# Two graph attention layers: another queue for one block's softmax sums, and a first node block in two parts

## The chip, the cores and the metric

The kernel runs on one core of a Trainium2 chip, in one launch. The metric is the device time of a run in microseconds (us); lower is better. All data are float32, except for a copy of the adjacency matrix that the kernel keeps in DRAM as one byte per element.

The engines are named as in the profile: PE is the matrix engine (PEld its weight loads), DVE the vector engine, ACT the scalar engine, POOL the GpSimd, SP the sync engine, which computes nothing here and issues transfers.

## The reference, cut to what matters

There are 4096 nodes with 512 features, and an adjacency matrix of 4096 x 4096. Two layers follow each other; H = 4 heads of D = 128 features each.

```python
# layer 0
h  = relu(layernorm(x))
Xw = einsum('hnd,hde->hne', heads(h), W)
f1, f2 = Xw . V[:, 0], Xw . V[:, 1]
att = softmax over neighbours of sigmoid(f1[:, :, None] + f2[:, None, :])
Xn  = batchnorm(att @ Xw)                       # the encoder's attention
emb = batchnorm(elu(Xn @ Wenc.T + b) + Xn)
Y   = elu((att @ emb_heads) @ W.T)              # the decoder's attention, the same weights
x   = x + batchnorm(elu(Y @ Wdec.T + b) + Y)
# layer 1
h     = relu(layernorm(x))
feats = einsum('nf,hfo->hno', h, W1)            # "the last layer's values"
e_s, e_n = feats . a_self, feats . a_neigh
attn  = softmax over neighbours of leaky_relu(e_s[:, :, None] + e_n[:, None, :])
x     = x + relu(attn @ feats + b)
```

A softmax's denominator is, for each target node, the sum of the unnormalized weights over its neighbours. The kernel multiplies unnormalized weights by the values and scales the result by the inverse of the denominator afterwards.

## The kernel before

**The encoder's attention.** Its function `attention` goes over 8 blocks: 4 heads times 2 halves of 2048 targets (`TB`). A block has 32 iterations `j`, one for each 128 source nodes. An iteration makes a tile `e` of 128 x 2048 weights: ACT computes a Tanh (L572) and an Exp (L573), DVE multiplies by the adjacency tile `a` (L574). PE then adds `e` times the values of these sources into four banks of PSUM (L470). The tile `a` is one byte per element and has five buffers; SP loads it (`load_mask`, L213) from the byte copy in DRAM, which eight large transfers on POOL's queue make out of the float adjacency (`copy_adjacency`, L603) while the features and the first block are computed.

**The sums.** The denominators of a block are collected in three ways, set for each block by a list of iterations: some weight tiles are summed on DVE into `acc` (L500), some are added by POOL's transfers into a second sum (L490), some go through PE against a tile of ones (L268). The first block (n = 0) uses no POOL transfers for sums. In the second block (n = 1) the iterations 12, 14, 17, 19, 22, 24 and 26 go by POOL.

**From sum to scale.** The denominators of a block are finished during the next block. `ending` puts its steps into that block's iterations with `at(j, ...)`: evict the products (`out_enc`), copy the sums out of PSUM and store them to DRAM (`denominators`, iteration 4: DVE L274, transfer L275), load them back as 128 columns of 16 (`columns`: transfer L280 into `dcol`), invert them on DVE (`invert_them`: L284, L285), store the inverses (`inverses`, L288), load them over all partitions (`spread`, L293), and scale (L688). In the encoder all these transfers are on POOL's queue (`hop = nc.gpsimd`). For the first block alone `slack` is 4, which puts the inversion and all after it four iterations later: the inversion in iteration 14.

**The order of the work.** The code's order is not the engines' order. A planner goes through the program with modelled durations and, for each engine, issues what is ready, the earlier in the program first; the order it finds is then fixed for each engine, and semaphores keep it right. `tc.issue_after(x)` holds instructions behind `x` on `x`'s own engine. The steps put in by `at` are held behind the weights of the iteration before (`pinned(products_of)`), whose last instructions are on ACT and DVE; a transfer issued by SP is not held by that. Each engine, SP and POOL included, takes its instructions strictly in the fixed order, and a transfer that reads what another wrote waits on its issuing engine until that one has landed.

**The last layer's values.** After the decoder's MLP, `residual(o, ib)` finishes 128 features `o` of 512 nodes `ib`: ACT scales (L870), DVE adds the input (L871). Sums over the features go into `S[ib]`. For the layernorm, PE multiplies `S` by a matrix of 1/512 (`mean_of`), which puts each node's mean on all partitions; `centred(ib)` subtracts it on DVE (L931), ACT takes the Relu (L935) and the squares (L934, L938), DVE adds the squares up (L939, L940), and `deviation` turns them into 1/std through PE again (L946). `values` multiplies the Relu by the weights `w1x`, 128 nodes at a time (L957). For the first 512 nodes (`ib == 0`) `S` holds three of the four feature blocks, and a second product adds the fourth (L919 and L920). Just before, PE does the small products of the weights with the attention vectors (L903) and, between them, four products that nobody reads (`stay_busy`, L121). `w1x`'s last columns are copied behind the residual (L922).

Of the kernel before, what the change touches and what calls it, by code (L numbers as in the profile page):

```python
# [31 lines left out]
FP = mybir.dt.float32  # L32
U8 = mybir.dt.uint8
AF = mybir.ActivationFunctionType
# [5 lines left out]
N, F, H, D, P = 4096, 512, 4, 128, 128  # L40
IB = 512
NIB = N // IB
NJ = N // P
C = IB // P
# [32 lines left out]
INVERT = 4  # L77
# [13 lines left out]
def kernel(ctx, tc, x, xT, adjT, w0, w0T, v0, wencT, wdecT, vecs, w1, w1T, a1, outT):  # L91
    nc = tc.nc
# [12 lines left out]
    def nodes(r, ib):  # L105
        return r[:, ib * IB:(ib + 1) * IB]
# [4 lines left out]
    def bank():  # L111
        return psum.tile([P, IB], FP, name="ps")

    def bank1():
        return psum1.tile([P, IB], FP, name="den")

    def stay_busy(behind, n=1, cols=IB):

        for _ in range(n):
            with tc.issue_after(behind.ins):  # L120
                behind = nc.tensor.matmul(bank()[:, 0:cols], ident, w0Ts.rearrange("p h d -> p (h d)")[:, 0:cols],  # L121
                                          start=True, stop=True)
        return behind
# [30 lines left out]
    bias = consts.tile([P, C], FP, name="bias")  # L154
# [69 lines left out]
    def attention(what, keep, pools, weights, values, row_of, out, finish, ebufs, modes=None, invert=None,  # L224
# [38 lines left out]
        hop = nc.scalar if kept is None else nc.gpsimd  # L263
# [4 lines left out]
                last_ones = nc.tensor.matmul(den[s * 32:(s + 1) * 32, :], ones[:, 0:32], t[:, s * IB:(s + 1) * IB],  # L268
                                             start=start, stop=stop)

        def denominators(h, tb, den):

            dsb = spool.tile([P, IB], FP, name="dsb", tag="rb", bufs=3)
            (nc.vector.tensor_copy if kept is not None else nc.scalar.copy)(dsb, den)  # L274
            hop.dma_start(dens[h][tb], dsb[0:P:32, :])  # L275

        def columns(h, tb, dcols):

            dcol = spool.tile([P, TB // P], FP, name="dcol", bufs=2)
            hop.dma_start(dcol, dens[h][tb].rearrange("s (q k) -> (s q) k", k=TB // P))  # L280
            dcols.append(dcol)
# [8 lines left out]
        def spread(h, tb, s):  # L290

            rb = spool.tile([P, IB], FP, name="rb", bufs=3 if fast is None else 2)
            hop.dma_start(rb, everywhere(rinvs[h][tb], 0, s * IB, IB))  # L293
            return rb

        def at(j, f, *args):

            later.setdefault(j, []).append(lambda: f(*args))

        def ending(h, tb, po, den, slack):  # L300

            outs = [out(spool, h, tb, s, po[s]) for s in range(SB)]
            if den is not None:

                dcols = []
                at(INVERT, denominators, h, tb, den)
                at(INVERT + (0 if hop is nc.gpsimd else 3), columns, h, tb, dcols)
                at(INVERT + slack + (6 if hop is nc.gpsimd else 7), invert_them, dcols)
                at(INVERT + slack + (6 if hop is nc.gpsimd else 10), inverses, h, tb, dcols)
            rbs = {}  # L310
            for s, o in enumerate(outs):

                j = INVERT + slack + (7 if hop is nc.gpsimd else 11) + s % 2 + s // 2 * (7 if hop is nc.gpsimd else 5)
                at(j, lambda s=s: rbs.update({s: spread(h, tb, s)}))
                for k, f in enumerate(finish):
                    at(j + (6 + k if hop is nc.gpsimd else 3 + 3 * k),
                       lambda f=f, s=s, o=o: f(spool, h, tb, s, o, rbs[s], False))
# [78 lines left out]
        for n, (h, tb) in enumerate(blocks):  # L396
            last = n == len(blocks) - 1
            moved, by_ones, *ends_later = modes(n) if modes is not None else ((), ())
            den = bank1() if invert is not None else None
# [135 lines left out]
            for s, b in enumerate(po):  # L535
                for part in last_parts(s):
                    for k, t in late:
                        nc.tensor.matmul(b[:, part], block(values[h], k), t[:, s * IB:(s + 1) * IB][:, part],
                                         start=(k == 0), stop=(k == NJ - 1 and part.stop == IB))
# [37 lines left out]
    a_att, b_att, a_mlp, b_mlp = (coefs[:, k, :] for k in range(4))  # L577

    with tc.tile_pool(name="keep", bufs=1) as keep:

        with tc.tile_pool(name="f_small", bufs=1) as small, tc.tile_pool(name="f_work", bufs=2) as work:
# [26 lines left out]
            for ib in range(NIB):  # L608
# [14 lines left out]
                hT = work.tile([P, C, IB], FP, name="hT")  # L623
                for c in range(C):
# [15 lines left out]
                    for fb in range(C):  # L640
                        last_pe = nc.tensor.transpose(pt[:, fb, :], hn[:, fb * P:(fb + 1) * P], ident)
                    nc.scalar.activation(hT[:, :, c * P:(c + 1) * P], pt, AF.Relu)
                if ib == 0:

                    pw = bank1()
                    with tc.issue_after(last_pe.ins):
                        for h in range(H):
                            nc.tensor.matmul(pw[:, 2 * h:2 * h + 2], w0Ts[:, h, :], v0s[:, h, :],
                                             start=True, stop=True)
# [4 lines left out]
                for c in range(C):  # L654
                    j = ib * C + c
                    for k in range(2):
                        pv = heads_of(bank())
                        for h in range(2):
                            nc.tensor.matmul(pv[:, h, :], hT[:, 2 * k + h, c * P:(c + 1) * P], w0x[:, 2 * k + h, :],
                                             start=True, stop=True)  # L660
# [196 lines left out]
    with tc.tile_pool(name="l_small", bufs=1) as small, tc.tile_pool(name="l_work", bufs=2) as work:  # L857
        x1 = [R[2]] + [small.tile([P, N], FP, name=f"x1_{o}") for o in range(1, C)]

        S = [small.tile([P, IB], FP, name=f"S{i}") for i in range(NIB)]  # L860
# [2 lines left out]
        a1s = small.tile([P, H, 2], FP, name="a1s")  # L863
        nc.scalar.dma_start(a1s, a1)

        def residual(o, ib):
            d = nodes(x1[o], ib)
            xt = work.tile([P, IB], FP, name="xt")
            nc.sync.dma_start(xt, xT[o * P:(o + 1) * P, ib * IB:(ib + 1) * IB])
            nc.scalar.activation(d, d, AF.Identity, bias=b_mlp[:, o:o + 1], scale=a_mlp[:, o:o + 1])  # L870
            added = nc.vector.tensor_add(d, d, xt)  # L871
            if o == 1:
                nc.gpsimd.tensor_add(S[ib], nodes(x1[0], ib), d)
            elif o == C - 2 or o == C - 1 and ib > 0:
                (nc.gpsimd if o < C - 1 else nc.vector).tensor_add(S[ib], S[ib], d)

            if o == C - 1:
                nc.sync.dma_start(nodes(outT[o * P:(o + 1) * P, :], ib), d)
            elif ib == NIB - 1:
                nc.sync.dma_start(outT[o * P:(o + 1) * P, :], x1[o])  # L880
            return added

        def between(o, ib, made):

            if o in (1, 2):
                residual(o - 1, ib)
            elif o == C - 1 and ib >= NIB // 2:
                residual(o - 1, ib - NIB // 2)
# [6 lines left out]
        for fb in range(C):  # L895
            nc.scalar.dma_start(w1x[:, fb, :, 0:D], w1[fb * P:(fb + 1) * P, :].rearrange("p (h d) -> p h d", d=D))
        pw = bank1()
        last_pe = last_product
        for fb in range(C):
            with tc.issue_after(last_pe.ins):  # L900
                for h in range(H):
                    k = 2 * (fb * H + h)
                    last_pe = nc.tensor.matmul(pw[:, k:k + 2], w1Ts[:, h, fb * P:(fb + 1) * P], a1s[:, h, :],  # L903
                                               start=True, stop=True)
            last_pe = stay_busy(last_pe)
        mean_of = small.tile([P, P], FP, name="mean_of")
        nc.gpsimd.memset(mean_of, 1.0 / F)
        vacc = edge.tile([P, H, D], FP, name="vacc")

        def centred(ib):  # L910

            if ib >= NIB // 2:
                residual(C - 2, ib)
            added = residual(C - 1, ib)
            pm = bank()
            if ib == 0:

                with tc.issue_after(last_pe.ins):
                    nc.tensor.matmul(pm, mean_of, S[ib], start=True, stop=False)  # L919
                nc.tensor.matmul(pm, mean_of, nodes(x1[C - 1], ib), start=False, stop=True)  # L920
                with tc.issue_after(added.ins):
                    nc.vector.tensor_copy(w1x[:, :, :, D:DX],  # L922
                                          pw[:, 0:2 * C * H].rearrange("p (c h s) -> p c h s", h=H, s=2))
            else:
                nc.tensor.matmul(pm, mean_of, S[ib], start=True, stop=True)
            hT = work.tile([P, C, IB], FP, name="hT")
            sq = work.tile([P, C, IB], FP, name="sq", bufs=1)

            d = hT if ib else sq
            for fb in range(C):  # L930
                nc.vector.tensor_sub(d[:, fb, :], nodes(x1[fb], ib), pm)  # L931
            for fb in range(C):
                if ib:
                    nc.scalar.activation(sq[:, fb, :], d[:, fb, :], AF.Square)  # L934
                last_relu = nc.scalar.activation(hT[:, fb, :], d[:, fb, :], AF.Relu)  # L935
            if ib == 0:
                for fb in range(C):
                    nc.scalar.activation(sq[:, fb, :], d[:, fb, :], AF.Square)  # L938
            nc.vector.tensor_add(sq[:, 0:2, :], sq[:, 0:2, :], sq[:, 2:4, :])  # L939
            nc.vector.tensor_add(S[ib], sq[:, 0, :], sq[:, 1, :])  # L940
            return hT, last_relu
# [19 lines left out]


        hT, last_relu = centred(0)
        ahead = [values(hT, c) for c in range(2)]
        with tc.issue_after(ahead[-1][1].ins):
            rstd = deviation(0)
        for ib in range(NIB):
            for c in range(C):

                if c == (1 if ib else 2) and ib < NIB - 1:  # L970
                    with pinned([last_relu]):
                        hT_next, last_relu = centred(ib + 1)
# [22 lines left out]
            if ib < NIB - 1:  # L995
                hT, rstd = hT_next, deviation(ib + 1)
        last_pe = stay_busy(pvs_last, cols=IB // 2)
# [4 lines left out]
        with tc.issue_after(last_pe.ins):  # L1002
            last_pe = stay_busy(nc.tensor.transpose(pt[0:H, 0:P], mloc, ident), cols=IB // 2)
# [4 lines left out]
        pm = bank1()  # L1008
        with tc.issue_after(last_pe.ins):
            last_pe = nc.tensor.matmul(pm[:, 0:H], ones[0:H, :], mdiag, start=True, stop=True)  # L1010
# [16 lines left out]
    with tc.issue_after(last_pe.ins):  # L1027
        for h in range(H):
            last_pe = nc.tensor.matmul(pss[:, h:h + 1], vacc[:, h, :], ones[:, 0:1], start=True, stop=True)
    last_pe = stay_busy(last_pe, 3)  # L1030
# [104 lines left out]
```

## Time and profile before

| | us |
|---|---|
| median of 3 runs | 3187.92 (3186.09 to 3189.45) |
| the profiled execution's own time | 3189.23 |
| its span, first to last instruction | 3187.4 |
| PE busy | 3140.5 (99%) |
| DVE busy | 2934.3 (92%) |
| ACT busy | 2572.8 (81%) |
| POOL busy | 522.3 (16%) |

The span is 1.8 us shorter than the profiled execution's time. Busy times are sums over the whole span, and PE's is an upper bound, since matmuls are pipelined. A row of groups gives a line of the code, its engine, its operation, what it writes and reads, and then its count, busy time, mean duration and the idle time before it with what ended that. SPq and ACTq are the engines' own queues, in which transfers are issued. The granted clock of PE was 0.998 of full speed.

### The profile page before, as it was taken

What the parts mean: (1) busy time and instruction counts of PE and PEld (TensorE: products, weight loads), DVE (VectorE), ACT (ScalarE), POOL (GpSimd) and SP (SyncE); (2) the same over time, 40 slices, a digit from 0 to 9 for tenths busy, and PEclk for the clock granted to TensorE, in tenths of its full rate; (3) what the DMA queues carried; (4) which work ended last, traced back from release to release, by engine and by line L of the source; (5) the groups of instructions that cost most, each with busy time, mean ns of one, the idle gap of its engine ahead of it and who ended that gap; (6) DMA issues with size and microseconds to landing.
All of it is one profiled execution on the core that took longest, in us unless ns stands there. A gap on an engine that the chain in (4) does not pass through costs nothing.

```text
span 3187.4 us, 30095 instructions
## 1 busy us (share of the span) xinstructions
PE 3140.5 (99%) x10555; PEld 1371.4 (43%) x10555; DVE 2934.3 (92%) x2222; ACT 2572.8 (81%) x1825; POOL 522.3 (16%) x679
## 2 busy tenths in 40 slices
PE   7999999999999999999999999999999999999999
PEld 6334444444444463333333333458644444444444
DVE  7989999999998778999999999785699999999998
ACT  7999999999998449999999999456755666665663
POOL 3001211211211000010100100026312222122221
PEclk9999999999999999999999999999999999999999
DMA  9998978988987014444445454331579999999996
GB/s 212 199 194 252 265 209 232 269 222 228 267 227 205 20 44 149 155 155 159 159 162 165 145 169 145 90 112 57 158 189 232 214 225 237 218 216 236 230 210 174
DMA packets 215488, 590.30 MB, mean 185 GB/s; under 512 B 25928, under 2 KB 29288, under 8 KB 199336
## 3 DMA queue, kind: packets, MB, share of 16 engines
q0 software_dynamic: 70976, 231.94, 38.1%
q1 hardware_dynamic: 132344, 332.53, 30.4%
q10 hardware_dynamic: 12016, 23.90, 2.1%
q8 instruction: 83, 1.36, 0.2%
q14 instruction: 69, 0.57, 0.1%
HBM read 379.20 MB, written 84.30 MB: 145 GB/s over the span
## 4 chain that ended last, share of the span: by engine, by line
PE 73%; DVE 10%; ACT 7%; issue 7%; DMA 2%; DVEq 0%; ACTq 0%; POOL 0%; POOLq 0%
PE ps L470 32%; PE ps L332 22%; PE ps L724 7%; ACT e L572 4%; DVE e L574 4%; PE den L332 3%; PE ps L957 3%; DVE acc L500 3%; ACT e L573 2%; PE den L268 2%; DMA a<-mask 1%; DVE R L500 1%; DVE e L1052 1%; PE ps L806 1%; PE ps L467 1%
## 5 line engine op out<-in xcount | busy, mean ns | idle before, releaser
L470 PE MATMUL ps<-e,R 128*128 128x512 f32 x3992 | 1736.0, 595 | 22.5 <-DVE e L574 18.5
L470 PEld LDWEIGHTS ps<-e,R 128*128 128x128 f32 x3992 | 754.3, 190 | 1000.4 <-issue 924.0
L574 DVE TENSOR_TENSOR e<-e,a 128x2048 f32<-128x2048 f32 (+1 forms) x470 | 1049.6, 2261 | 77.7 <-ACT e L573 64.3
L572 ACT ACTIVATE e<-rowb,score 128x2048 f32<-128x2048 f32 (+1 forms) x470 | 909.0, 1969 | 20.2 <-PE ps L332 9.0
L573 ACT ACTIVATE e<-e 128x2048 f32<-128x2048 f32 (+1 forms) x470 | 866.6, 1879 | 8.3 <-DVE e L574 5.0
L332 PE MATMUL ps<-e,R 128*64 128x512 f32 x2624 | 746.8, 592 | 1.6 <-DVE e L574 1.5
L1051 ACT ACTIVATE e<-rowb,nq,jcol 128x2048 f32<-128x2048 f32 x224 | 459.3, 2088 | 264.1 <-DMA w<-e 137.1
L1052 DVE SCALAR_TENSOR_TENSOR e<-e,jcol,a 128x2048 f32<-128x2048 f32 (+1 forms) x265 | 591.2, 2262 | 2.8 <-ACT e L1051 2.8
L332 PEld LDWEIGHTS ps<-e,R 128*64 128x64 f32 x2624 | 241.9, 137 | 319.8 <-issue 316.2
L500 DVE TENSOR_TENSOR R<-R,e 128x2048 f32<-128x2048 f32 x124 | 282.2, 2276 | 0.0
L500 DVE TENSOR_TENSOR acc<-acc,e 128x2048 f32<-128x2048 f32 x122 | 278.6, 2284 | 1.0
L490 POOL DMA_DIRECT2D w<-e x178 | 149.1, 847 | 610.7 <-DMA w<-e 301.0
L724 PE MATMUL ps<-R,w 128*128 128x512 f32 x512 | 220.8, 592 | 0.6 <-DVE w L698 0.6
L490 POOL DMA_DIRECT2D acc<-e x142 | 119.1, 895 | 517.7 <-DMA acc<-e 199.1
L724 PEld LDWEIGHTS ps<-R,w 128*128 128x128 f32 x512 | 97.1, 190 | 123.0 <-issue 116.5
L332 PE MATMUL den<-e,R 128*64 128x512 f32 x320 | 149.8, 592 | 0.0
L332 PE MATMUL ps<-e,w 128*64 128x512 f32 x288 | 138.1, 592 | 0.7 <-DVE e L574 0.7
L293 POOL DMA_DIRECT2D rb<-rinvs x60 | 34.2, 573 | 519.3 <-DVE R L688 455.2
L957 PE MATMUL ps<-w1x,hT 128*128 128x260 f32 x512 | 115.5, 384 | 1.4 <-ACT hT L935 1.4
L332 PE MATMUL ps<-t,w 128*64 128x512 f32 x336 | 111.2, 592 | 1.0 <-DVE t L341 1.0
L957 PEld LDWEIGHTS ps<-w1x,hT 128*128 128x128 f32 x512 | 96.5, 190 | 19.9 <-issue 3.3
L332 PE MATMUL ps<-t,R 128*64 128x512 f32 x192 | 90.2, 592 | 0.0
(206 smaller groups left out, 2112.9 us busy)
## 6 DMA issues: line engine op xcount, KB each, us to landing
a<-mask SPq DMA_DIRECT2D x720, 256.0 KB, 4.2
w<-e POOLq DMA_DIRECT2D x178, 512.0 KB, 6.5
acc<-e POOLq DMA_DIRECT2D x142, 512.0 KB, 6.9
e<-ekeep SPq DMA_DIRECT2D x48, 1024.0 KB, 5.0
ekeep<-e SPq DMA_DIRECT2D x36, 1024.0 KB, 7.5
mask<-in_adjT POOLq DMA_DIRECT2D x8, 2048.0 KB, 107.3
rowb<-rows SPq DMA_DIRECT2D x16, 1024.0 KB, 7.2
rb<-rinvs POOLq DMA_DIRECT2D x60, 256.0 KB, 4.2
```

Of the source, the lines that this page charges most:

```text
L268: last_ones = nc.tensor.matmul(den[s * 32:(s + 1) * 32, :], ones[:, 0:32], t[:, s * IB:(s + 1) * IB], start=start, stop=stop)
L332: last_half = nc.tensor.matmul(b[g * HD:(g + 1) * HD, :], weight, x, start=start, stop=stop)
L470: last_main = nc.tensor.matmul(b, block(values[h], j), e[:, s * IB:(s + 1) * IB], start=(j == 0), stop=(j == NJ - 1))
L490: nc.gpsimd.dma_start(into_half, e_half, **({"accum_op": ALU.add} if j > moved[0] else {}))
L500: nc.vector.tensor_add(acc, acc, e)
L572: nc.scalar.activation(e, rowb, AF.Tanh, bias=column(score[:, 1], j, h), scale=0.5)
L573: last_act = nc.scalar.activation(e, e, AF.Exp, scale=0.5)
L574: last_dve = nc.vector.tensor_mul(e, e, a)
L724: last = nc.tensor.matmul(z, w[:, fb, o * P:(o + 1) * P], nodes(src[fb], ib), start=(fb == 0), stop=(fb == C - 1))
L957: m = nc.tensor.matmul(banks[k][:, 0:2 * DX], hT[:, fb, c * P:(c + 1) * P], w1x[:, fb, 2 * k:2 * k + 2, :].rearrange("p h x -> p (h x)"), ...
L1051: last_act = nc.scalar.activation(e, rowb, AF.Relu, bias=column(nq, j, h), scale=column(jcol, j, h))
L1052: last_dve = nc.vector.scalar_tensor_tensor(e, e, column(jcol2, j, h), a, ALU.add, ALU.mult)
```

## The change

It has two parts that have nothing to do with each other.

The first concerns the denominators of the encoder's first block, the only one with `slack`. Their store and their load go to SP's queue (`nc.sync`) instead of POOL's, and the load is put two iterations later (`slack // 2`), into iteration 6. The inversion stays in iteration 14, and the store of the inverses and their spread stay on POOL.

The second concerns the first 512 nodes of the last layer's values. The residual of the last feature block, the second product of the mean, the subtraction and the Relu are done in parts of 128 and 384 nodes. The product of `S` goes ahead, into a bank of its own, in the place of the first of the four products that nobody reads; the matrix `mean_of` is set earlier.

```diff
-        def denominators(h, tb, den):
+        def denominators(h, tb, den, hop):
...
-        def columns(h, tb, dcols):
+        def columns(h, tb, dcols, hop):
...
-                at(INVERT, denominators, h, tb, den)
-                at(INVERT + (0 if hop is nc.gpsimd else 3), columns, h, tb, dcols)
+                at(INVERT, denominators, h, tb, den, nc.sync if slack else hop)
+                at(INVERT + (0 if hop is nc.gpsimd else 3) + slack // 2, columns, h, tb, dcols, nc.sync if slack else hop)
...
-        def residual(o, ib):
+        def residual(o, ib, parts=(slice(0, IB),)):
...
-            nc.scalar.activation(d, d, AF.Identity, bias=b_mlp[:, o:o + 1], scale=a_mlp[:, o:o + 1])
-            added = nc.vector.tensor_add(d, d, xt)
+            for p in parts:
+                nc.scalar.activation(d[:, p], d[:, p], AF.Identity, bias=b_mlp[:, o:o + 1], scale=a_mlp[:, o:o + 1])
+                added = nc.vector.tensor_add(d[:, p], d[:, p], xt[:, p])
...
         pw = bank1()
+        pm0 = bank()
+        mean_of = small.tile([P, P], FP, name="mean_of")
+        nc.gpsimd.memset(mean_of, 1.0 / F)
         last_pe = last_product
         for fb in range(C):
...
-            last_pe = stay_busy(last_pe)
-        mean_of = small.tile([P, P], FP, name="mean_of")
-        nc.gpsimd.memset(mean_of, 1.0 / F)
+            if fb == 0:
+                with tc.issue_after(last_pe.ins):
+                    last_pe = nc.tensor.matmul(pm0, mean_of, S[0], start=True, stop=False)
+            else:
+                last_pe = stay_busy(last_pe)
...
-            added = residual(C - 1, ib)
-            pm = bank()
+            parts = (slice(0, IB),) if ib else (slice(0, P), slice(P, IB))
+            added = residual(C - 1, ib, parts)
             if ib == 0:
-
+                pm = pm0
                 with tc.issue_after(last_pe.ins):
-                    nc.tensor.matmul(pm, mean_of, S[ib], start=True, stop=False)
-                nc.tensor.matmul(pm, mean_of, nodes(x1[C - 1], ib), start=False, stop=True)
+                    for p in parts:
+                        nc.tensor.matmul(pm[:, p], mean_of, nodes(x1[C - 1], ib)[:, p], start=False,
+                                         stop=(p.stop == IB))
...
             else:
+                pm = bank()
                 nc.tensor.matmul(pm, mean_of, S[ib], start=True, stop=True)
...
-            for fb in range(C):
-                nc.vector.tensor_sub(d[:, fb, :], nodes(x1[fb], ib), pm)
-            for fb in range(C):
-                if ib:
-                    nc.scalar.activation(sq[:, fb, :], d[:, fb, :], AF.Square)
-                last_relu = nc.scalar.activation(hT[:, fb, :], d[:, fb, :], AF.Relu)
+            for p in parts:
+                for fb in range(C):
+                    nc.vector.tensor_sub(d[:, fb, p], nodes(x1[fb], ib)[:, p], pm[:, p])
+                for fb in range(C):
+                    if ib:
+                        nc.scalar.activation(sq[:, fb, :], d[:, fb, :], AF.Square)
+                    last_relu = nc.scalar.activation(hT[:, fb, p], d[:, fb, p], AF.Relu)
```

## The prediction

> **What bounds the kernel now.** I read the page first: PE is busy 99% of the span, DVE 92%, ACT 81%, but these are means over stages. So I went to the two stretches that the change touches: 193 to 325 us (end of block 0 and block 1 of the encoder's attention) and 2127 to 2264 us (the last layer's values).
>
> In the first stretch, busy time by window (columns after the window: its length, then busy us and instructions of PE, PEld, DVE, ACT, POOL, then granted clock, DMA share, GB/s):
>
> ```profile
> 193.00:244.00 51.00, 51.00 (x171) 20.13 (x170) 43.99 (x24) 48.34 (x27) 0.60 (x1) 1.00 1.04 194
> 244.00:248.00 4.00, 4.00 (x11) 1.80 (x10) 1.14 (x3) 3.39 (x2) 1.63 (x3) 1.00 0.64 189
> 248.00:325.00 77.00, 73.19 (x189) 30.57 (x187) 76.97 (x45) 72.74 (x40) 13.61 (x18) 0.98 0.86 242
> ```
>
> From 248 us DVE has no idle time, so whatever DVE loses before 248 is lost for the block. What it loses is in the table of its waits from 193 to 248 us (total, times, longest):
>
> ```profile
> DVE e L574 <- DMA a<-mask: 7.4, 6, 2.7
> DVE dcol L284 <- DMA dcol<-dens: 2.9, 1, 2.9
> ```
>
> The second line is the change's target. The chain of waits shows it as one story (start, us, what):
>
> ```profile
> 205.36 0.61 DVE dsb L274
> ...
> 206.62 0.60 POOL dens L275
> 207.22 37.32 issue
> ...
> 244.56 3.08 DMA dcol<-dens
> ...
> 247.66 0.06 DVE dcol L284
> ```
>
> POOL issues the store at 206.62 and stands 37 us for its landing. The transfers of 190 to 244 us say why (KB each, median us from issue to landing):
>
> ```profile
> a<-mask SPq DMA_DIRECT2D x14, 256.0 KB, 15.0
> ekeep<-e ACTq DMA_DIRECT2D x2, 1024.0 KB, 10.1
> dens<-dsb POOLq DMA_DIRECT2D x1, 8.0 KB, 37.7
> ```
>
> 8 KB need 37.7 us because on POOL's queue they stand behind the eight casts of the adjacency (L603: the last issued at 51.8 us, the longest landing 192.2 us, so near 244 us). But on SP's queue a mask load needs 15.0 us too. SP issues these masks one by one as DVE frees a buffer:
>
> ```profile
> 205.39 0.32 SPq L213 DMA_DIRECT2D a<-mask  x1
> ...
> 210.39 0.32 SPq L213 DMA_DIRECT2D a<-mask  x1
> ...
> 212.59 0.32 SPq L213 DMA_DIRECT2D a<-mask  x1
> ```
>
> In the second stretch PE idles 1.44 us in all, before its first product, and the chain there is:
>
> ```profile
> 2133.81 0.96 PE ps L121 x2
> 2134.77 0.86 PE ps L919 x2
> 2135.63 0.87 PE ps L920 x2
> 2136.50 0.03 issue
> 2136.53 0.70 DVE sq L931
> 2137.22 0.02 issue
> 2137.25 0.64 ACT hT L935
> 2137.89 0.04 issue
> 2137.93 7.31 PE ps L957 x32
> ```
>
> After 2138 PE works 125.83 of 126 us, so a product that starts earlier there moves the end by as much.
>
> **What the Trainium skill says.** "DMA: Bandwidth & Descriptors", section "Queues, rings and completion order": each DMA engine takes turns between queues by packet and works off one queue's ring in order. The trace agrees: 37.7 us behind casts, 15.0 us behind other masks. The same page, "Two DMAs through the same engine are not ordered": a transfer that reads what another wrote must be held back by its issuing engine until the first has landed. POOL's 37.32 us is that; SP will do the same. "PSUM — Partial Sum Buffer", section "PSUM bank collisions raise a hardware error": a bank is to be guarded as a whole, not by address. No row of before shows two engines on parts of one bank, so this decides a bound below.
>
> **Part one, the denominators of block 0.** Removed from POOL: the store (0.60 us) and the load (0.59 us), and with them POOL's stand. Added to SP: the same two issues, near 0.3 us each as a mask's. The store waits for the copy L274, done at 205.97. SP is idle then (205.39 to 210.39), so the store costs the masks nothing but four 2 KB packets. Its landing is unknown; it enters rings in which, with 15.0 us each and one landing every 3.5 to 4 us, about four mask loads stand, so I take their 15.0 us: 206.3 + 15.0 = 221.3. Ends: 3 us (the dcol load took 3.08 us when the casts were done) and 37.7 us.
>
> The load is the dearer half. It is put two iterations later in the program, but ahead of the masks of iteration 9 on, which SP issues from 210.39; and the planner, reckoning a short landing, finds SP with nothing else to do. So I place it directly behind the store, and SP stands 206.6 to 221.3. Queued behind it: the masks issued at 210.39, 212.59, 215.51 and 220.52 before. Four earlier masks are in flight, and DVE lives on them until it begins iteration 9 at 226.09. Then the rings have run dry: with 221.6 for the dcol load, 222.0 for the first mask, about 2 us until its packets move and 1 us for the dcol packets ahead, then 3.5 us at the pace at which masks land (DVE took them 222.64, 226.09), I get 228.5 instead of 226.1: DVE 2.4 us late. Its waits in 226 to 244.8 sum to 1.16 + 0.48 us, of which the first is what lengthens; it makes up little. At 244.8 DVE no longer stands 2.86 us. Net 2.4 - 2.9 = **-0.5 us**. Ends: -2.9 (SP's hold costs nothing) and, for a landing some 2 us later than taken, +1.5. DVE's order after 248, the inversion (0.17 + 0.24 us) and the two later steps on POOL (rinvs, rb) stay. POOL's accumulates at 245.14 can go up to 2.7 us sooner; none waits for them there.
>
> **Part two, the first 512 nodes.** One filler pair (0.96 us) becomes the S product (0.86): PE reaches the x product at 2134.67 instead of 2135.63. The x product is two pairs instead of one: 0.87 + 0.1 for two more starts (estimate). S of the first 512 nodes is ready: POOL's last add into it ran from 2110.87 to 2112.14. The parts of L870 (0.81 us whole) and L871 (0.69) end near 2134.5 with one more start each, under the fillers; L922 (0.18) follows under the x product. If fillers were gone, these would be the chain, 0.2 us longer than before. By the PSUM rule the subtraction waits for both parts: 2135.65. For 128 columns I use "VectorE: DVE Perf Modes", section on the TRN2 errata: (128+151)/0.96 = 0.29 us on DVE and (224+128)/1.2 = 0.29 us on ACT; its 0.69 and 0.61 for 512 agree with 0.69 (L931) and 0.62 (L935) here. First product: 2135.65 + 0.03 + 0.29 + 0.02 + 0.29 + 0.04 = 2136.32 against 2137.93, -1.6 us. The 384-column parts end by 2138.9, before PE has done the 3.5 us of the first 128 nodes. Added: four subtractions and four Relus more, some 0.1 us of start each, on engines that had waited 2.00 and 3.54 us. Next in line is L946, which needs S again after the squares: written at 2144.1 before, read at 2145.08, so 1.0 us of the gain is safe; the squares come some 0.6 us sooner, so I take **-1.4 us**. Ends: -1.0, and -2.2 if DVE may read the first part while PE writes the second (0.65 us less).
>
> **Sum.** -0.5 - 1.4 = -1.9 us. The profiled execution took 3189.23 us (span 3187.4, 1.8 around it), 1.3 above the median of 3187.92. On it: 3187.3; on the median: **3186.0 us**. 0.2% is 6.4 us (3181.5 to 3194.3), about what a measurement of this kernel can tell from no change.
>
> **Rivals.** *The hold is hidden*: the planner puts the load behind the masks of iterations 9 and 10, or the store lands sooner, so the rings don't dry; only the dcol packets count (1 us, half taken by waits). Then -2.0 - 1.4: 3184.5. For it: the load's shift by two iterations; against: SP's gap at 206. *Nothing arrives*: SP's hold costs the whole 2.9 us and L946 stands for S: -1, 3187. *More than the parts*: the masks' waits of 7.4 us shrink as well, say by 2, with both upper ends: -2.9 - 2.2 - 2 = -7.1, 3180.8. For it: DVE and ACT are both near full and stand for each other (ACT 5.0 us for DVE); against: no mask buffer is added. *The hold runs dry*: the store lands as late as on POOL. From a landing of 223 us on each us costs DVE one; over 229 us the kernel is slower by more than 0.2%; at 244 us DVE would begin iteration 9 near 247 instead of 226: +21 - 2.9 - 1.4, 3205. For it: rings are shared with the casts; against: 15.0 us for masks 32 times as large.
>
> **Chances.** Forecast 0.44, hidden hold 0.25, nothing 0.10, more 0.15, dry 0.06. Only "more" is faster by over 0.2%, only "dry" slower: 0.15, 0.79, 0.06. The range takes forecast, hidden and nothing with their ends (-5.1 to +0.5 us) and 1.3 us of scatter: 3181.5 to 3188.8.
>
> **What would show it.** dens on SP lands 12 to 17 us after issue; no DVE wait on dcol; one mask wait of 2 to 4 us near 228; dcol's inversion near 247; PE's idle time before L957 near 0.7 us and L957 beginning 1.6 us sooner after L186. A dens landing under 8 us, or masks issued between store and load, makes part one worth more; an L931 that starts before the second x product ends makes part two 2 us.

## The result, and the profile after

The changed kernel takes 3192.24 us (median of 21 runs, 3190.03 to 3196.12) against 3187.62 us of the kernel before on the same chip (21 runs). The ratio is 1.0015, with a 95% interval of 1.0009 to 1.0022: about 4.6 us slower. That is less than 0.2%, but an equal time lies outside the interval, and the measured time lies 3.4 us above the upper end of the forecast range. The profiled execution took 3193.17 us, with a span of 3191.4.

Line numbers up to L574 are those of before. The last layer's have moved: ACT's scaling is L871, DVE's add L872, the small products L907, the product of S L911, that of x L926, the subtraction L940, the Relu L944, the values L966, the products for 1/std L955.

**Part one.** DVE's table of waits of the kernel after, from 193 to 248 us (total, times, longest):

```profile
DVE e L574 <- DMA a<-mask: 13.9, 5, 8.2
```

The wait for dcol (2.9 us) is gone, as the change meant it to be; it doesn't come back up to 260 us either. The wait for masks, 7.4 us with a longest of 2.7 before, is 6.5 us longer, and it has one stand of 8.2 us. SP's table of waits, 190 to 260 us, has what stands in front of it:

```profile
SPq L280 <- DMA dens<-dsb: 15.3, 1, 15.3
SPq L213 <- DMA a<-mask: 10.5, 5, 7.8
```

and SP's timeline from 200 to 240 us the order (start, us, line, transfer):

```profile
208.01 0.62 SPq L275 DMA_DIRECT2D dens<-dsb  x1
223.93 0.32 SPq L280 DMA_DIRECT2D dcol<-dens  x1
224.35 13.40 SPq L213 DMA_DIRECT2D a<-mask  x6
```

No mask is issued for over 16 us, from 207.67 to 224.35. The masks of iterations 9 to 12, which the kernel before issued at 210.39, 212.59, 215.51 and 220.52, now leave one behind the other from 224.35, with the next one behind them. The chain of waits shows the price:

```profile
222.45 1.90 DVE acc L500
224.35 10.67 DMA a<-mask
235.02 0.03 issue
...
235.11 2.30 DVE e L574
...
253.06 0.09 DVE dcol L284
```

DVE ends the sums of iteration 8 at 224.35 and has nothing to multiply by until mask 9 lands at 235.02. Iteration 9 starts at 235.11; before, at 226.09. This execution began its first weight tile 1.81 us later (65.48 instead of 63.67, its first loads took longer), so 7.2 us of the 9.0 belong to the change. Busy time by window of the kernel after (window, length, then busy us and instructions of PE, PEld, DVE, ACT, POOL, granted clock, DMA share, GB/s):

```profile
222.00:227.20 5.20, 5.20 (x25) 1.75 (x23) 4.91 (x3) 5.20 (x3) 0.00 (x0) 1.00 1.06 117
227.20:230.00 2.80, 2.80 (x10) 1.25 (x7) 0.00 (x0) 2.80 (x3) 0.00 (x0) 1.00 1.11 109
230.00:235.00 5.00, 5.00 (x13) 2.28 (x12) 0.00 (x0) 1.10 (x1) 0.00 (x0) 1.00 1.06 162
```

and the same windows of the kernel before:

```profile
222.00:227.20 5.20, 5.20 (x24) 1.90 (x20) 4.04 (x3) 5.20 (x4) 0.00 (x0) 1.00 1.06 161
227.20:230.00 2.80, 2.80 (x8) 1.31 (x7) 2.77 (x2) 1.55 (x2) 0.00 (x0) 1.00 1.07 162
230.00:235.00 5.00, 5.00 (x18) 1.82 (x21) 4.52 (x3) 5.00 (x4) 0.00 (x0) 1.00 1.04 233
```

The DMA share reads full in all six rows and hides the matter; GB/s tells it. The casts still run here, in the middle of block 1. With hardly a mask in the rings, 109 to 117 GB/s move, nearly all of it the casts'. DVE's column is 0.00 in the two stretches from 227.2 to 235. The DMA view of the second window names what went through (queue: packets, MB, share of 16 engines; q0 is POOL's with the casts, q1 SP's):

```profile
q0 software_dynamic: 145, 0.30, 104.3%
q1 hardware_dynamic: 135, 0.01, 7.2%
```

135 packets of SP's queue with 0.01 MB: they are the 128 pieces of 64 bytes of the dcol load. For 2.8 us SP's queue gets nearly as many turns as the casts (135 to 145) and moves no mask with them.

**Part two.** The chain of the kernel after, to be laid beside that of before at 2133.81:

```profile
2137.00 0.97 PE ps L121 x2
2137.97 0.79 PE den L907 x8
2138.75 0.96 PE ps L121 x2
2139.72 0.88 PE ps L926 x4
2140.60 0.03 issue
2140.63 0.30 DVE sq L940
2140.93 0.02 issue
2140.95 0.32 ACT hT L944
2141.27 0.04 issue
2141.31 7.29 PE ps L966 x32
2148.60 1.03 PE den L955 x8
```

The product of S is out of this chain, and the subtraction and the Relu take 0.30 and 0.32 us where they took 0.70 and 0.64. PE's wait in the table of waits went from 1.4 to 0.7:

```profile
PE ps L966 <- ACT hT L944: 0.7, 1, 0.7
```

From the end of L186 (the coefficients of the residual; 2137.81, before 2132.87) to the first product it is 3.50 us instead of 5.06, so 1.56 us less. L955 follows the 32 products without a wait.

### The profile page after: what moved, and what is told of

Its sections match the earlier page's. It is cut to its first block, busy times and chain, and to the rows that moved or that the text cites. A ratio compares the mean times of both kernels' runs of the same rounds, so it can differ in the third digit from the quotient of the medians.

```text
span 3191.4 us, 30104 instructions
## 1 busy us (share of the span) xinstructions
PE 3140.4 (98%) x10555; PEld 1370.9 (43%) x10555; DVE 2935.1 (92%) x2227; ACT 2574.4 (81%) x1830; POOL 521.5 (16%) x677
## 3 DMA queue, kind: packets, MB, share of 16 engines
q8 instruction: 83, 1.36, 0.2%
## 4 chain that ended last, share of the span: by engine, by line
PE 74%; DVE 9%; ACT 6%; DMA 5%; issue 5%; POOL 0%; DVEq 0%; ACTq 0%; SPq 0%; POOLq 0%
PE ps L470 33%; PE ps L332 22%; PE ps L724 7%; PE den L332 3%; PE ps L966 3%; ACT e L572 3%; DVE e L574 3%; DMA a<-mask 3%; DVE acc L500 2%; ACT e L573 2%; DMA acc<-e 2%; PE den L268 2%; DVE R L500 1%; PE ps L806 1%; DVE e L1061 1%
## 5 line engine op out<-in xcount | busy, mean ns | idle before, releaser
L574 DVE TENSOR_TENSOR e<-e,a 128x2048 f32<-128x2048 f32 (+1 forms) x470 | 1049.2, 2260 | 85.8 <-ACT e L573 68.8
L500 DVE TENSOR_TENSOR R<-R,e 128x2048 f32<-128x2048 f32 x124 | 281.9, 2273 | 0.0
L500 DVE TENSOR_TENSOR acc<-acc,e 128x2048 f32<-128x2048 f32 x122 | 278.5, 2283 | 1.0
L966 PE MATMUL ps<-w1x,hT 128*128 128x260 f32 x512 | 115.5, 384 | 0.7 <-ACT hT L944 0.7
L966 PEld LDWEIGHTS ps<-w1x,hT 128*128 128x128 f32 x512 | 96.6, 190 | 18.8 <-issue 3.4
```

Of the source, the lines that this page charges most:

```text
L500: nc.vector.tensor_add(acc, acc, e)
L574: last_dve = nc.vector.tensor_mul(e, e, a)
L966: m = nc.tensor.matmul(banks[k][:, 0:2 * DX], hT[:, fb, c * P:(c + 1) * P], w1x[:, fb, 2 * k:2 * k + 2, :].rearrange("p h x -> p (h x)"), ...
```

## Experiments

Each kernel was timed over five rounds beside the kernel before, unless noted; ratios are to that. "Iteration 14" is the start of L574 of iteration 14 in block 1, counted from the start of the first weight tile of block 0, so that executions which started late can be compared. In the kernel before it lies at 184.11, 181.52 and 182.33 us in three profiled executions, in p2_only, which has the same code up to there, at 181.90, and in the kernel after at 187.58.

**Each part alone.** p1_only has the change of `denominators`, `columns` and the two lines in `ending`, p2_only all the rest.

```diff
# p1_only, against before
-                at(INVERT, denominators, h, tb, den)
-                at(INVERT + (0 if hop is nc.gpsimd else 3), columns, h, tb, dcols)
+                at(INVERT, denominators, h, tb, den, nc.sync if slack else hop)
+                at(INVERT + (0 if hop is nc.gpsimd else 3) + slack // 2, columns, h, tb, dcols, nc.sync if slack else hop)
# p2_only: residual(o, ib, parts), pm0 before the loop, parts in centred
```

> Part one alone: store and load of block 0's denominators on SP's queue, the last layer as before. Theory 'dry rings': SP waits for the store's landing and keeps back four mask loads, the rings run empty, and iteration 9 of block 1 begins some 7 us late, of which some 3.5 are left after the inversion; with part two's gain of 1.4 gone, 5 to 6 us slower than before in all if the measured 4.6 us are to be explained, at least 3.5. Theory 'start': the difference lies in the first loads of x (1.8 us later in the changed kernel's profile) and in chance; then part one is within 2 us of before. DVE's one long wait on a mask at iteration 9 near 8 us under 'dry rings', in either case no wait on dcol.

> Part two alone: the last layer's first 512 nodes in parts, the denominators on POOL as before. From L186 (the last coefficient) to the first product of the values: 3.5 us as in the changed kernel, 5.06 before. 1.3 to 1.6 us faster than before, 3186.2. If part two had a hidden cost (its extra instructions, a bank taken earlier), it would be 0 or slower, and the stage from L186 to the first weights of the last layer would be over 135 us (before 136.0, changed kernel 134.7).

Measured: p1_only 3193.42 us (12 runs) against 3186.73, ratio 1.0020 [1.0011, 1.0028]; p2_only 3186.08 (13 runs), ratio 0.9997 [0.9989, 1.0005]. The slowdown is part one's; at 6.7 us it is a little more than the 5 to 6 expected. DVE's waits of p1_only from 193 to 250 us are those of the whole change:

```profile
DVE e L574 <- DMA a<-mask: 13.7, 5, 8.0
```

Part two's gain is too small for the measured times, but not for the trace: from the start of L186's last instruction to the first weight tile of the last layer it is 136.21, 136.22 and 136.21 us in the three executions of the kernel before, and 134.86 in p2_only and in the kernel after. That is 1.36 us.

**The stand and the small pieces apart.** Two things hold up mask 9: SP stands, and then the load of dcol has 128 pieces to pass. hold_only leaves SP the stand and takes the pieces away: SP stores the sums, then loads the same 8 KB in four rows into a tile that nobody uses, and the real dcol goes on POOL's queue. dummy_share is the opposite: a load of 128 pieces of 64 bytes, of an input, with nothing to wait for.

```diff
# hold_only
+            spare = spool.tile([SB, IB], FP, name="spare", tag="rb", bufs=3)
+            nc.sync.dma_start(spare, dens[h][tb])
# dummy_share
+            spare = spool.tile([P, TB // P], FP, name="dcol", bufs=2)
+            nc.sync.dma_start(spare, x[0:4, :].rearrange("s (q k) -> (s q) k", k=TB // P))
# both
+                at(INVERT, denominators, h, tb, den, nc.sync if slack else hop)
+                at(INVERT + (0 if hop is nc.gpsimd else 3), columns, h, tb, dcols, hop)
+                if slack:
+                    at(INVERT + 2, ...)
```

> Store on SP, load of dcol on POOL, and on SP, where the change has the load, a load that nobody needs: the same 8 KB in four pieces of 2 KB into a spare tile. SP waits for the store as in the change, but the 128 pieces of 64 bytes are not in the masks' rings. Theory 'dry rings': the wait and the restart of the empty rings remain (3.3 us from issue to the first packet), the 2.6 us of small packets go: iteration 9 of block 1 waits 5 to 6 us for its mask instead of 8.0 to 8.2, and the kernel is 3 to 4.5 us slower than before (part one alone: 6). Theory 'share': as fast as store_sp, within 1 us, and no wait over 3 us on a mask.

> Store on SP, load of dcol on POOL, and on SP behind the store a load that nobody needs, of 128 pieces of 64 bytes from the input x: it waits for nothing, so SP is not held, but the same small packets stand in the masks' rings. Theory 'dry rings': masks of iterations 9 to 12 are issued as DVE frees their buffers; they come at most 2.6 us later: iteration 9 waits 2 to 4 us, and the kernel is between equal to before and 2 us slower. Theory 'share': 4 to 6 us slower than before as in part one alone, with iteration 9 waiting near 8 us.

Measured: hold_only 3192.88 us (20 runs) against 3187.35, ratio 1.0017 [1.0010, 1.0024]; dummy_share 3190.62 (21 runs), ratio 1.0010 [1.0003, 1.0016]. The chain of hold_only from 215 to 240 us (L581 and L507 are L574 and L500, moved by the added lines):

```profile
221.37 2.04 DVE acc L507
223.41 8.55 DMA a<-mask
...
232.06 2.30 DVE e L581
```

and DVE's waits from 193 to 250 us, first hold_only's,

```profile
DVE e L581 <- DMA a<-mask: 12.0, 5, 6.2
```

then dummy_share's:

```profile
DVE e L581 <- DMA a<-mask: 9.8, 5, 3.9
```

The longest wait is that ahead of iteration 9. It is 1.16 us in the kernel before, 6.23 in hold_only (+5.1), 3.93 in dummy_share (+2.8) and 7.99 in p1_only (+6.8). Both causes are real: by 'share' alone hold_only would have been as fast as store_sp, and by the stand alone dummy_share as fast as before. Together they come to 7.9, 1.1 us more than when they occur at once. The stand is the larger by nearly two to one. Both kernels lost more time than their expectations allowed (5.5 us against 3 to 4.5, and 3.3 against 2 at most), though the intervals, some 4 to 5 us wide, reach into these ranges.

**SP without a stand.** store_sp moves only the store; POOL loads. late_load moves both, but puts the load behind the mask of iteration 12, where the store has nearly landed.

```diff
# both
+                at(INVERT, denominators, h, tb, den, nc.sync if slack else hop)
# store_sp
+                at(INVERT + (0 if hop is nc.gpsimd else 3), columns, h, tb, dcols, hop)
# late_load, in the loop over iterations ahead of the step's mask load
+                if slack:
+                    late_columns[13] = lambda: columns(h, tb, dcols, nc.sync)
...
+                if n == 1 and j in late_columns:
+                    with pinned([a_load]):
+                        late_columns.pop(j)()
```

> Store of block 0's denominators on SP's queue, the load on POOL's as before: SP waits for nothing. Theory 'dry rings': masks come as before (no wait over 3 us on a mask), the store lands in some 15 us, POOL issues the load near 222 us and it lands behind the casts near 244; the inversion is no longer waited for by more than 1 us: 2 to 3 us faster than before. Theory 'share' (what costs is the denominators' own packets among the masks): only four packets are there, so the same 2 to 3 us faster. Theory 'no value' (DVE's 2.9 us wait was slack): no difference from before.

> Part one with the load's place on SP set by hand: behind the mask load of iteration 12 instead of behind that of iteration 8; by then the store has landed, so SP waits little. Theory 'dry rings': no mask wait over 3 us at iterations 9 to 12, dcol lands near 238 us, no wait on dcol: 1.5 to 3 us faster than before. Theory 'share': the 128 packets of 64 bytes of the load still take 2.6 us of the rings' turns among the masks, only later, so masks from iteration 13 on come 2.6 us later and little or nothing is gained; part one would be as slow as in the changed kernel if its packets were the cause.

Measured: store_sp 3186.83 us (13 runs), ratio 0.9998 [0.9989, 1.0006]; late_load 3187.26 (13 runs), ratio 1.0001 [0.9993, 1.0009]. Neither can be told from before, though in both the only DVE wait of 193 to 250 us is that for masks. In store_sp it is

```profile
DVE e L574 <- DMA a<-mask: 7.4, 6, 2.7
```

SP's waits of late_load, 190 to 260 us, have 1.2 us on the store instead of 15.3:

```profile
SPq L280 <- DMA dens<-dsb: 1.2, 1, 1.2
```

late_load also sends the 128 pieces through SP's queue. They are issued at 222.56, stand behind the masks that are already there, and move between 236.9 and 241.2 us by the times of their packets, while the casts come to their end. Here nobody waits longer for the masks behind them: DVE's waits stay at 7.1 us. So the pieces cost DVE nothing where no mask is due behind them. Iteration 14 starts at 180.91 and 180.77 us. Both kernels were expected to be 1.5 to 3 us faster. The medians show nothing of it, as in 'no value', though the intervals, which reach down to -3.5 and -2.2 us, don't exclude it all.

**What the wait for dcol is worth.** If it is worth 2.9 us, store_sp and late_load should have shown it. slack5 takes the wait away and moves no transfer: the inversion comes one iteration later.

```diff
-                   4 if kept == "write" and n == 0 else 0)
+                   5 if kept == "write" and n == 0 else 0)
```

> The queues stay as in the kernel before (denominators of block 0 stored and loaded on POOL's queue); only their inversion and the two steps after it are put one iteration later (slack 5 instead of 4). No transfer moves. Theory 'the wait on dcol is worth what one execution showed': -2.9 us. Theory 'the wait is small in most executions and DVE's later work takes back most of it': DVE's wait on dcol is 0 and the kernel is 0 to 1 us faster, not to be told from before.

The kernel before was profiled twice more, unchanged, with one execution each:

> The kernel before, unchanged, for a second profile of it. In its first profile DVE waited 2.86 us for dcol; in p2_only, which has the same code there, 0.91 us. Theory 'chance in the first profile': the casts end at a nearly fixed time after the start, while the first weight tile came 1.1 us sooner in that profile (63.67 against 64.75 us), so a late start shortens this wait: 0.5 to 2.5 us here, and the less, the later the first weight tile. Theory 'fixed': 2.9 us again.

> The kernel before once more: DVE's wait on dcol, 2.86 us in the first profile and 0.51 in the second, comes to something between 0 and 3 us; the casts end near 243 us from the span's start again, and the wait is the smaller the later block 0 started.

Measured: slack5 3186.84 us (13 runs) against 3187.27, ratio 1.0000 [0.9992, 1.0008], with no wait for dcol and iteration 14 at 181.14. The single runs of before took 3185.70 and 3186.39 us. The line of DVE's waits that the forecast was built on, in before_again and then in before_third (190 to 260 us):

```profile
DVE dcol L284 <- DMA dcol<-dens: 0.5, 1, 0.5
```

```profile
DVE dcol L284 <- DMA dcol<-dens: 1.2, 1, 1.2
```

p2_only, which leaves this part as it was, has 0.91 us. So of four executions the first profile, with 2.86, was the dearest, and the mean is 1.4. 'Fixed' is out. What slack5 was expected to show, that DVE's later work takes back most of the wait, is out as well: from the start of iteration 14 to that of block 2 these four take 68.86 to 68.87 us, whatever the wait was. Up to block 2 the wait is worth its own length, but it is short in most executions. The expectation that the wait is the smaller the later block 0 started doesn't hold strictly: with the first weight tile at 63.67, 64.05, 64.13 and 64.75 us it was 2.86, 1.18, 0.51 and 0.91. The store's landing differs too, 37.7 us in the first and 35.8 to 36.4 in the other three, and so does the load's, 3.1 us and 2.4 to 2.5. Why is not shown.

**The best of both.** Part two, with SP's store and POOL's load (store_sp_p2), and with SP's store and the late load on SP (late_load_p2).

```diff
# store_sp + p2_only; late_load + p2_only
```

> Part two as in the change, with the store of block 0's denominators on SP and the load left on POOL: the two pieces that cost nothing together. If the two parts add up as p1_only and p2_only do (6.2 - 1.3 against 4.6 us for both), store_sp (0.85 us faster by its mean) and p2_only (1.3 us) give 2.1 us faster than before, 3184.6; 1 to 4 us. If POOL's load behind the casts matters, 1 us less.

> Store of block 0's denominators on POOL's queue as before or SyncE's as in late_load, their load on SyncE's queue only after the store has landed (put ahead of the mask that is issued near 222 us), so that SyncE never stands; and part two as in the change. If the gains add, late_load's -0.1 and part two's -1.3 us give about -1.4 us: 3186, within 0.2% of before.

Measured: store_sp_p2 3186.24 us (13 runs) against 3187.35, ratio 0.9997 [0.9989, 1.0005]; late_load_p2 3185.75 (13 runs) against 3187.27, ratio 0.9995 [0.9987, 1.0004]. Both are faster than the change: their intervals end below 1.0009, where its own begins. By the medians store_sp_p2 is 1.1 us faster than before, at the lower end of what was expected, and late_load_p2 1.5, as expected. That they beat the kernel before is likely from the trace (1.36 us of part two, iteration 14 at 181.17 and 180.81) but not shown by the times.

## Why the prediction was wrong

**Right.** The order on SP: the load goes directly behind the store and SP stands between them, ahead of masks 9 to 12. The landing of dens: 15.9 us, forecast 15.0. The mechanism of the stand, a longer first mask wait with little made up later: block 2 of the kernel after begins 6.1 us later than in before_again, as iteration 14 had (3.5 us later than in the first profile, with its longer wait for dcol). All of part two: -1.56 us at the first product (forecast -1.6), PE's wait 0.7, and 1.36 us kept at the end (forecast 1.4). The end of -2.2 us, in which DVE reads the first part while PE writes the second, is out: L940 begins at 2140.63, after both x products end at 2140.60. That agrees with the rule by which the forecast decided this, in the Trainium skill's "PSUM — Partial Sum Buffer", section "PSUM bank collisions raise a hardware error", to guard a bank and not an address; what would happen without that order no run here shows.

**The step that failed first** is "I get 228.5 instead of 226.1: DVE 2.4 us late". On the clock of before (after's times less 1.81 us) the sum and the trace compare so:

| term | forecast, us | measured, us |
|---|---|---|
| store landed, load issued | 221.6 | 222.1 |
| first packet of dcol (2.0 after the mask's issue; measured 3.3 after the load's) | 224.0 | 225.5 |
| dcol's packets through (1.0; 2.6) | 225.0 | 228.1 |
| mask 9 landed (3.5; 5.1) | 228.5 | 233.2 |
| iteration 9 late by | 2.4 | 7.2 |

The store landed 0.5 us later than forecast, the first packet took 1.0 us longer, the pieces 1.6 and the mask 1.6: four errors, all in the same direction.

The first packet was priced at 2 us, for which the forecast showed no row. The trace of before has the price of a start under the casts. ACT's store of `ekeep` is issued at 210.39 into a queue with nothing in it. The DMA view from 210.4 to 213.9 us has no packet of that queue (q10); the view from 213.9 to 214.3 has the first:

```profile
q10 hardware_dynamic: 11, 0.09, 53.1%
```

That is 3.5 us, and the same at 228.42. In the kernel after an `ekeep` store issued at 237.43, where the casts are nearly done, has its first packet at 239.20, after 1.8 us. So the 3.3 us of dcol's load is what a start into an empty queue takes beside the casts in these traces, and the forecast's 2 us is near what it takes without them.

The dcol term was priced by its bytes. Its 128 pieces are priced by turns: a piece of 64 bytes waits for a packet of a cast (322 ns: 104.3% of 16 engines' 2.8 us, over 145 packets) as one of 2 KB does, and eight pieces on each of 16 engines at that give 2.6 us. A mask of 256 KB is 128 pieces too, of 2 KB, so the 8 KB of dcol need nearly as many turns as a mask. "DMA: Bandwidth & Descriptors" in the Trainium skill, section "Queues, rings and completion order", has engines take turns by packet, and I had cited that sentence; I did not use it for the small transfer. The page's typical packet holds 9 to 17 descriptors, here each piece counts as a packet of its own (128 of the 135).

The mask term was priced by the pace at which masks land while several are in flight, which is no price for the first into empty rings: hold_only, without the pieces, needs 8.55 us from issue to landing where the forecast had 2 + 3.5. The packets of mask 9 itself pass from 230.0 to 233.2 us; SP's queue in the DMA view of the kernel after from 229.9 to 233.2:

```profile
q1 hardware_dynamic: 139, 0.26, 23.6%
```

The other 1.8 us lie between its last packet and its landing at 235.02. In the kernel before there are 1.8 us as well (the 0.26 MB of mask 9 have passed by 224.3, it lands at 226.02). So a start of 3.3 us stood ahead of the first packets and an end of 1.8 us behind the last. In a running stream the packets of other masks pass meanwhile, and the pace of landings doesn't show them.

**The second** is "At 244.8 DVE no longer stands 2.86 us". It was so in the first profile, but three executions had 0.5 to 1.2, and store_sp, late_load and slack5, all without the wait, are each within 0.1% of before; the intervals of late_load and slack5 end at -2.2 and -2.5 us, short of -2.9. The size was read from one execution and used as the typical one, although that execution was 1.3 us above the median.

**The sum** that the runs give: part one lengthens the waits for masks by 6.3 to 6.5 us (6.8 to 7.0 at iteration 9, less 0.5 at iteration 11, where DVE no longer waits), less the dcol wait, 1.4 in the mean, and part two -1.4: about +3.6. The kernel measured +4.6, with an interval of 2.9 to 7.0. From the runs alone, +0.20% and -0.03% are +5.4 us.

**The rivals.** *The hold runs dry* named the right mechanism, but put its price on a landing of 223 us or later; with a landing near the forecast one (222.1 on the clock of before) DVE was already 7.2 us late. *The hold is hidden* is what late_load does: its order removes the stand, as argued, but brings -0.1 to +0.1% and not 2.0 us, since the wait it removes is small. The range's upper end was set by one mishap (a landing 2 us later) and not by the restart, which needed bounds of its own. It was also added up wrongly: +0.5 us and 1.3 us of scatter on 3187.9 are 3189.7, not 3188.8. The measured 3192.24 lies above both.

## What to carry to other kernels

A transfer that must wait for another is only as cheap as the queue that waits: move the store freely, but put the dependent load where the store has landed, or on a queue with nothing behind it. Price a small scattered load by its pieces times the packets it takes turns with. Price the first transfer into an empty queue from its issue to its landing, read from another queue's first transfer under the same load, never by the pace of a stream that is already running. A wait of a few us that depends on when another stream ends should be read from several executions before a gain is built on it.

## What the runs showed of the hardware that was not expected

A first transfer into an empty queue took 3.2 to 3.6 us from issue to first packet while the casts kept the DMA engines busy (SP's in the kernel after, p1_only and hold_only, ACT's in the kernel before and store_sp), and 1.6 us after them (ACT's store of `ekeep` issued at 248.06 in store_sp).

The granted clock of PE has short half-rate stretches. In the first profile of before, by window (columns as above, the clock third from the right):

```profile
281.00:284.30 3.30, 1.40 (x4) 0.68 (x4) 3.30 (x3) 3.30 (x3) 1.09 (x2) 1.00 0.71 205
284.00:288.00 4.00, 4.00 (x7) 1.66 (x6) 4.00 (x3) 3.69 (x2) 0.95 (x2) 0.57 1.00 221
```

A mean of 0.57 over 4 us is 3.4 us at 0.5, and PE has 7 products there where before_again, at full clock, has 10. The stretches come at a handful of places, and which of them an execution has differs: this one near 284, 929 and 2267 us, the kernel after near 72 and 191.5, before_again none of these. "TensorE: Matmul & The Clock Gate" in the Trainium skill, section "What's actually happening", has a gate that halves PE's clock after an idle window of about 3.4 us. The length and the half rate agree. The idle window doesn't: PE was busy 1.40 of the 3.30 us ahead of 284 us, and 3.40 of the 3.40 us ahead of 929 (926.0 to 929.4), if its busy time, which is an upper bound, can be trusted there. Each stretch can cost up to 1.7 us of PE, so they may be part of why single executions of one kernel differ by some us; no run tested it.

A load of 8 KB in 128 pieces, sent where masks were due (dummy_share), cost DVE 2.8 us, while a store of the same 8 KB in four rows ahead of the same masks (store_sp) left the waits for them at the 7.4 us of before.
